# A graph network in four layers on one core: the third layer's convolution reads the adjacency as f32 strips for three query blocks at a time

## The chip, the core and the metric

The kernel runs on one NeuronCore of a Trainium2 chip. The engines are TensorE (PE, matmuls; PEld is its weight load), VectorE (DVE), ScalarE (ACT), GpSimd (POOL) and SyncE (SP); the last issues most of the transfers, and POOL issues those that change the type of the data. All transfers share the core's 16 DMA engines. The metric is the device time of one execution in microseconds (us); less is better. Three executions of the kernel before took 2046.96, 2052.23 and 2040.15 us.

## The reference

Four layers act on x (4096 nodes, 128 features) with one adjacency matrix adj (4096 x 4096, f32, symmetric, zeros and ones, ones on the diagonal). After each layer stands `x = layernorm(x + layer(x, adj))`.

Layer 0 is a hyperbolic layer with sigmoid attention, layer 1 a transformer convolution with four heads. The change is in layer 2, the third layer:

```python
def _L2_gnn_ref(x, adj, weight):
    n = adj.shape[0]
    adj_hat = adj + jnp.eye(n, dtype=adj.dtype)
    deg = jnp.sum(adj_hat, axis=1)
    d_inv_sqrt = (deg + 1e-08) ** (-0.5)
    support = d_inv_sqrt[:, None] * adj_hat * d_inv_sqrt[None, :]
    out = jnp.matmul(jnp.matmul(support, x), weight)
    return jax.nn.relu(out)
```

Layer 3 is a graph attention: `H = X @ W.T + b`, a score s_i + r_j for each edge, leaky_relu, softmax over the neighbours and `att @ H`. Layers 2 and 3 are in one function of the kernel, `layers23`.

## The kernel before

N is 4096, P is 128 (the partitions), S is 512 (a query block), NS = 8 blocks of nodes, NT = 32 tiles of 128 nodes, D = 128 features. X holds the features of all nodes in SBUF, node tiles on partitions. The order of a run is: layer 0 (0 to 700 us; in it `narrow`, L1917, writes a bf16 copy of adj, `adjb`, to DRAM by transfers of POOL that cast), completing the copy (to 790), layer 1 (to 1590), the convolution of layer 2 (to 1789), and layer 3, whose first block is `attend_first` (to 1829) and whose other seven are `attend_factored` (to the end).

`adjb` is stored in blocks of 512 x 512; `block(I, J)` is 128 partitions x 4 x 512 in bf16, 0.52 MB. The kernel takes fast paths that hold only if all entries of adj are zero or one. So it searches adj itself for other values: L1985 does this in layer 1 and `look` (L2336) in layer 2, each writing one column of marks per call (`mark`, up to MARKS columns). If a mark is set at the end, the whole net is run again by a general class; with these inputs it is not.

**The convolution.** Y holds the nodes scaled by deg^-1/2 in f32. `split` (L2353 on ACT, L2355 on DVE) takes it apart into three bf16 parts, each the rounded rest of the one before, for four tiles at a time. For a query block I and a block J of nodes, `convolve` (L2372) does 4 x 3 matmuls: node tile j of a part is the weights (128 x 128), the 512 columns of the adjacency block are the moving data, and everything is added up in one PSUM tile `pa` per query block. The order is I by I: 64 groups g = (I, J), each with one ring load from `adjb` on SP (`load`, L2322, ring of 8 blocks, seven ahead). The identity of `adj + I` is added by `diagonal` (L2346) to the block on the diagonal in the ring, or for the first block by identity matmuls (L2364).

The search is done beside it on f32 data of its own: `wide` (L2331) loads 1 MB halves of a strip of 128 rows of adj on SP into a pool `rot` of two buffers, and `look` is one instruction of 128 x 2048 on DVE, with every second group.

**The end of a query block** is `finish(I)`, a generator that is advanced one step a group beside the next query block: copy of the PSUM tile on ACT (L2401), the product with the weight on PE (pb, L2405), relu and scale on ACT (L2408), residual and layer norm on DVE (L2410 to L2419), transposes on PE (pt, L2425), and the scores of layer 3 (psr, L2443, `rho`, `col`, and the scaled features F, on PE, DVE and ACT). The sums over the own scores go over DVE (`urr`, L2432), in the last block over a matmul.

**The first attention block**, `attend_first`: for each of 32 node tiles one DVE instruction makes w from rho, col and the adjacency block (L2384), and an f32 matmul adds it to pa (L2387). It needs F and col of tile j, so the `finish` of block 7 must end before tiles 28 to 31; `close_first` gathers the sums and the marks. All this is inside `manual_schedule`, so each engine's order is the order of the program's text; SP and POOL take their issues in that order, and an issue that must wait for a buffer holds up those behind it on its queue.

The PSUM tiles are in pools `ps_b`, `ps_t`, `ps_s` and `ps_a` with two buffers each.

## Time and profile before

| | us |
|---|---|
| three executions, median | 2046.96 (2040.15 to 2052.23) |
| the profiled execution, its own time | 2050.21 |
| its span, first to last instruction | 2048.4 |
| layer 0, 0 to 700 | 700 |
| completing the bf16 copy, 700 to 790 | 90 |
| layer 1, 790 to 1590 | 800 |
| convolution of layer 2, 1590 to 1789 | 199, PE busy 187.2, DVE 147.9, DMA share 0.93 |
| first attention block, 1789 to 1829 | 40, PE busy 36.0, DVE 30.9, DMA share 0.36 |
| other seven blocks, 1829 to 2048 | 219, PE busy 207.5, DVE 185.5, DMA share 0.38 |

A line of the profile's groups reads: line of the kernel, engine, operation, what it writes and reads, shapes, count, then busy time in us and the mean ns of one, then the idle time of the engine ahead of them and what ended it. A line of a stretch reads: from and to, its length, busy time of PE, PEld, DVE, ACT and POOL with the number of instructions, the granted clock of TensorE as a share of full speed, the busy share of the 16 DMA engines, and the GB/s that they moved. The busy share of transfers can be over 1, since a packet's time counts while it waits. A line of the DMA issues gives the queue, how many, the size of one and the median time from issue to landing.

### The profile page before, as it was taken

To read this page: it belongs to the slowest core of one execution; us is meant where nothing else is said; L and a number is where in the kernel's file an instruction comes from. 1 tells how busy PE (TensorE), PEld (TensorE's weight loads), DVE (VectorE), ACT (ScalarE), POOL (GpSimd) and SP (SyncE) were. 2 spreads that over 40 slices of the span, in tenths; PEclk is the share of its full clock that TensorE was granted. 3 is DMA by queue.
4 is the path that set the end of the run, shared out by engine and by line. 5 is a ranking of instruction groups with operands and counts; after the bars stand their busy time and mean duration, and the time that the engine had idled before them with its cause. 6 is when DMAs were issued, how large, how long until landed. Compare 5 with 4: busy or idle time off the path is not lost.

```text
span 2048.4 us, 23818 instructions
## 1 busy us (share of the span) xinstructions
PE 1900.9 (93%) x8648; PEld 978.9 (48%) x8680; DVE 1736.6 (85%) x2685; ACT 1328.8 (65%) x1681; POOL 171.4 (8%) x269
## 2 busy tenths in 40 slices
PE   4789999999997788999999999999999799999997
PEld 4257766666666454333333333333333344444443
DVE  6579999998988946789999999999999777778986
ACT  5589999999997723777787777778787322210000
POOL 2211112111100221300000000000000000000000
PEclk8569999999999998999999999999999999999999
DMA  3488989899825977853535453545343799934441
GB/s 101 49 139 147 155 167 157 155 163 168 144 93 191 363 277 223 199 152 132 144 124 146 136 150 134 144 133 155 124 139 118 290 396 373 340 116 156 155 148 43
DMA packets 138064, 350.22 MB, mean 171 GB/s; under 512 B 13196, under 2 KB 56364, under 8 KB 125648
## 3 DMA queue, kind: packets, MB, share of 16 engines
q1 hardware_dynamic: 82944, 230.27, 32.3%
q0 software_dynamic: 45632, 50.69, 20.1%
q10 hardware_dynamic: 9360, 67.64, 9.9%
q8 instruction: 70, 1.15, 0.2%
q14 instruction: 58, 0.48, 0.1%
HBM read 371.54 MB, written 44.12 MB: 203 GB/s over the span
## 4 chain that ended last, share of the span: by engine, by line
PE 49%; DVE 24%; ACT 16%; DMA 6%; issue 4%; SPq 0%; POOL 0%; another core or an unknown queue 0%; ACTq 0%; DVEq 0%; POOLq 0%
PE pv L2020 11%; PE pa L1573 9%; DVE e L2003 9%; PE pa L2372 7%; PE ps L1994 6%; ACT e L2001 4%; PE pz L1775 3%; DMA up<-adjb 3%; DVE nat L1985 2%; ACT w L1792 2%; PE pi L1859 2%; PE pj L1874 2%; ACT s L1815 2%; ACT y L1811 2%; ACT y L1807 1%
## 5 line engine op out<-in xcount | busy, mean ns | idle before, releaser
L2003 DVE SCALAR_TENSOR_TENSOR e<-at,e 128x2048 f32<-128x2048 bf16 x256 | 582.6, 2286 | 77.3 <-ACT e L2001 76.7
L2001 ACT ACTIVATE e<-ps 128x1024 f32<-128x1024 f32 x512 | 492.9, 1024 | 150.6 <-PE ps L1994 121.6
L2020 PE MATMUL pv<-e,VA 128*64 128x512 f32 x2048 | 497.6, 607 | 6.7 <-DVE e L2003 5.7
L1994 PE MATMUL ps<-QS,KS 128*128 128x512 f32 x1024 | 314.8, 425 | 9.1 <-ACT e L2001 8.5
L1994 PEld LDWEIGHTS ps<-QS,KS 128*128 128x128 f32 x1024 | 170.9, 189 | 236.5 <-ACT e L2001 177.4
L2020 PEld LDWEIGHTS pv<-e,VA 128*64 128x64 f32 x2048 | 125.1, 136 | 250.2 <-issue 214.4
L1573 PE MATMUL pa<-w,Y 128*128 128x512 f32 x448 | 195.3, 594 | 0.0
L1775 PE MATMUL pz<-HT 128*128 128x512 f32 x288 | 171.8, 681 | 15.0 <-DVE w L1847 10.2
L1570 DVE SCALAR_TENSOR_TENSOR w<-rho,col,ring 128x512 f32<-128x512 f32 x224 | 162.7, 746 | 22.3 <-PE pa L1573 9.7
L2372 PE MATMUL pa<-ring,Y 128*128 128x512 bf16 x750 | 172.7, 384 | 8.7 <-ACT Y L2353 6.7
L1859 PE MATMUL pi<-HA,w 128*128 128x129 f32 x1152 | 156.6, 286 | 6.5 <-ACT s L1815 5.3
L1859 PEld LDWEIGHTS pi<-HA,w 128*128 128x128 f32 x1152 | 143.3, 199 | 18.2 <-issue 10.2
L1573 PEld LDWEIGHTS pa<-w,Y 128*128 128x128 f32 x448 | 83.8, 190 | 105.9 <-issue 80.3
L1976 ACT ACTIVATE nat<-nat 128x2048 f32<-128x2048 f32 x64 | 122.6, 1915 | 2.8 <-DMA nat<-in_adj_dram 2.8
L1874 PE MATMUL pj<-HA,w 128*128 128x129 f32 x896 | 120.7, 293 | 3.4 <-DVE X L1888 2.4
L2372 PEld LDWEIGHTS <-Y 128*128 128x128 bf16 x768 | 75.4, 99 | 100.9 <-ACT Y L2353 9.7
L1784 DVE TENSOR_SCALAR t<-pz 128x512 f32<-128x512 f32 x144 | 93.6, 682 | 30.2 <-PE pz L1778 30.2
L1874 PEld LDWEIGHTS pj<-HA,w 128*128 128x128 f32 x896 | 112.8, 205 | 11.2 <-issue 6.8
L1823 DVE SCALAR_TENSOR_TENSOR t<-t,s 128x2048 f32<-128x2048 f32 x36 | 82.3, 2286 | 13.4 <-ACT s L1815 13.4
L1792 ACT ACTIVATE w<-di,dr 128x512 f32<-128x512 f32 x144 | 90.6, 707 | 1.5 <-DMA di<-rows 1.5
L2336 DVE SCALAR_TENSOR_TENSOR nat<-nat 128x2048 f32<-128x2048 f32 x32 | 73.1, 2287 | 20.5 <-DMA nat<-in_adj_dram 20.5
L1847 DVE TENSOR_TENSOR w<-w,ptz 128x512 f32<-128x512 f32 x112 | 73.4, 681 | 18.7 <-PE ptz L1842 17.3
(410 smaller groups left out, 2343.1 us busy)
## 6 DMA issues: line engine op xcount, KB each, us to landing
nat<-in_adj_dram ACTq DMA_DIRECT2D x64, 1024.0 KB, 5.1
ring<-adjb SPq DMA_DIRECT2D x128, 512.0 KB, 4.7
ad<-in_adj_dram SPq DMA_DIRECT2D x36, 1024.0 KB, 9.4
adjb<-in_adj_dram POOLq DMA_DIRECT2D x64, 512.0 KB, 11.4
nat<-in_adj_dram SPq DMA_DIRECT2D x32, 1024.0 KB, 7.5
at<-adjb SPq DMA_DIRECT2D x63, 512.0 KB, 3.5
low<-adjb SPq DMA_DIRECT2D x36, 512.0 KB, 5.1
up<-adjb SPq DMA_DIRECT2D x28, 512.0 KB, 6.6
```

What stands on the lines that cost most here:

```text
L1570: nc.vector.scalar_tensor_tensor(w, rho[:, I * S : (I + 1) * S], col[:, 0, j : j + 1], at[:, jb, :], op0=ALU.max, op1=ALU.mult)
L1573: nc.tensor.matmul(pa, lhsT=F[:, j, :], rhs=w, start=False, stop=(j == NT - 1), skip_group_check=True)
L1775: nc.tensor.matmul(pz, lhsT=HT[:, j * P : (j + 1) * P], rhs=HT[:, I * S : (I + 1) * S], start=True, stop=False)
L1792: nc.scalar.activation(w[:, jb, :], st[p]["d"][k], AF.Sigmoid, bias=dr[:, 4 * J + jb : 4 * J + jb + 1])
L1859: nc.tensor.matmul(row[I, "po"][ib // 2][:, ib % 2, :], lhsT=st[p]["w0"][:, jb, ib * P : (ib + 1) * P], rhs=HA[:, 4 * J + jb, :], start=False,
L1874: nc.tensor.matmul(pj[:, a, :], lhsT=st[p]["w1"][:, ib, jb * P : (jb + 1) * P], rhs=HA[:, 4 * I + ib, :], start=(ib == 0), stop=(ib == 3),)
L1976: nc.scalar.activation(nat, nat, AF.Identity, accum_out=self.deg2[:, k, i : i + 1])
L1994: nc.tensor.matmul(p[:, h, :], lhsT=KS[:, h2 + h, jb * P : (jb + 1) * P], rhs=QS[I % 2][:, h2 + h, :], start=True, stop=True,)
L2001: nc.scalar.activation(e[:, h2 : h2 + 2, :], p, AF.Exp)
L2003: nc.vector.scalar_tensor_tensor(e, at[:, jb % 4, :].unsqueeze(1).to_broadcast([P, NH, S]), 0.0, e, op0=ALU.not_equal, op1=ALU.mult,)
L2020: nc.tensor.matmul(st["po"][h // 2][g : g + 64, :], lhsT=VA[:, o : o + 64], rhs=e[:, h, :], start=(jb == 0), stop=(jb == NT - 1), skip_gro ...
L2372: nc.tensor.matmul(st["pa"], lhsT=parts[k][:, j, :], rhs=at[:, jb, :], start=(I > 0 and j == k == 0), stop=(j == NT - 1 and k == 2), skip_ ...
```

## The change

The convolution no longer reads `adjb`. It reads adj itself, in strips: 128 rows of f32 and the columns of three query blocks (128 x 1536; in the last pass, with two query blocks, 128 x 1024), cast to F32R (a type in which TensorE takes f32 data with one matmul) by a transfer of POOL, `fetch`. There are three passes over the 32 row tiles, with query blocks 0 to 2, 3 to 5, and 6 and 7, 96 strips in all, in seven slots of which six are loaded ahead. A strip serves two parts of the nodes (F32R, `split` with two parts instead of three) and two or three query blocks, whose sums are in as many PSUM tiles (`ps_a` has four buffers now, `ps_b` and `ps_t` one).

The search uses the same strips: `look` runs two strips ahead of the matmuls on half of them (row tiles with j % 4 < 2, the same rows as before), and writes its unused result to a tile `junk` in bf16. The diagonal is added to the strip in the slot, 128 x 128. `wide`, `diagonal` and the identity matmuls are gone.

At the end of a pass the `finish` of two or three query blocks are opened together, and `proceed` advances one step a strip: the first alone, then the two at the head of the list by turns. After the last pass those of blocks 6 and 7 run beside `attend_first`, which goes tile by tile now; both of them take the sums by a matmul. The ring has six buffers, and its loads for the attention are issued in the last pass.

```diff
@@ -1643,7 +1643,7 @@
 
 class Fast(Net):
 
-    MARKS = 112
+    MARKS = 160
 
 
 
@@ -2250,7 +2250,9 @@
 
         nc, tc, N, NT, NS, D, X = self.nc, self.tc, self.N, self.NT, self.NS, self.D, self.X
         with ExitStack() as ctx:
-            RING = 8
+            RING, SLOTS = 6, 7
+            passes = [(0, 3), (3, 6), (6, 8)]
+            W = 3 * S
             ring = ctx.enter_context(tc.tile_pool(name="ring", bufs=1)).tile([P, RING, 4, S], BF16, tag="ring", name="ring")
             keep = ctx.enter_context(tc.tile_pool(name="keep3", bufs=1))
             pctx = ctx.enter_context(ExitStack())
@@ -2264,14 +2266,14 @@
             a0 = keep.tile([P, S], F32, tag="a0", name="a0")
             pre = pctx.enter_context(tc.tile_pool(name="pre3", bufs=1))
             rot = pctx.enter_context(tc.tile_pool(name="rot2", bufs=2))
+            slots = [pre.tile([P, W], F32R, tag=f"row{k}", name=f"row{k}") for k in range(SLOTS)]
+            junk = pre.tile([P, W], BF16, tag="junk", name="junk")
             wp = pctx.enter_context(tc.tile_pool(name="w2", bufs=4))
-            ps_b = pctx.enter_context(tc.tile_pool(name="ps_b", bufs=2, space=PSUM))
-            ps_t = pctx.enter_context(tc.tile_pool(name="ps_t", bufs=2, space=PSUM))
+            ps_b = pctx.enter_context(tc.tile_pool(name="ps_b", bufs=1, space=PSUM))
+            ps_t = pctx.enter_context(tc.tile_pool(name="ps_t", bufs=1, space=PSUM))
             ps_s = pctx.enter_context(tc.tile_pool(name="ps_s", bufs=2, space=PSUM))
-            ps_a = pctx.enter_context(tc.tile_pool(name="ps_a", bufs=2, space=PSUM))
-            parts = [pre.tile([P, NT, D], BF16, tag=f"Y{k}", name=f"Y{k}") for k in range(3)]
-            identb = pre.tile([P, P], BF16, tag="identb", name="identb")
-            nc.vector.tensor_copy(identb, self.ident)
+            ps_a = pctx.enter_context(tc.tile_pool(name="ps_a", bufs=4, space=PSUM))
+            parts = [pre.tile([P, NT, D], F32R, tag=f"Y{k}", name=f"Y{k}") for k in range(2)]
             w = self.load_mat(w2, "w2")
             br = self.load_row(bias, "br3", keep)
             wn = self.load_mat(weight, "wn3", pre)
@@ -2318,32 +2320,35 @@
                 nc.vector.memset(tot[:, D - 1 : D], float(N))
                 nc.vector.memset(eps, TINY)
 
-            def load(g):
-                nc.sync.dma_start(out=ring[:, g % RING, :, :], in_=self.block(g // NS % NS, g % NS))
+            def load(q):
+                nc.sync.dma_start(out=ring[:, q % RING, :, :], in_=self.block(q // NS, q % NS))
+
+            strips = [(lo, hi, j) for lo, hi in passes for j in range(NT)]
+
+            def fetch(n):
+
+                if n < len(strips):
+                    lo, hi, j = strips[n]
+                    nc.gpsimd.dma_start(
+                        out=slots[n % SLOTS][:, 0 : (hi - lo) * S], in_=self.adj[j * P : (j + 1) * P, lo * S : hi * S]
+                    )
 
             def open_sums():
                 return ps_a.tile([P, S], F32, tag="pa", name="pa")
 
-            def wide(n):
-
-                i, k = n // 4 * 4 + n // 2 % 2, n % 2
-                nat = st["nat", n] = rot.tile([P, N // 2], F32, tag="nat", name="nat")
-                nc.sync.dma_start(out=nat, in_=self.adj[i * P : (i + 1) * P, k * N // 2 : (k + 1) * N // 2])
-
             def look(n):
 
-                nat = st.pop(("nat", n))
-                nc.vector.scalar_tensor_tensor(
-                    nat, nat, 0.0, nat, op0=ALU.not_equal, op1=ALU.not_equal, accum_out=self.mark()
-                )
-
-            def diagonal(I):
-
-
-                at = ring[:, (NS * I + I) % RING, :, :]
-                for b in range(4):
-                    a = at[:, b, b * P : (b + 1) * P]
-                    nc.vector.tensor_tensor(a, a, identb, ALU.add)
+                lo, hi, j = strips[n]
+                a = slots[n % SLOTS]
+                if j % 4 < 2:
+                    w = (hi - lo) * S
+                    nat = a[:, 0:w].bitcast(F32)
+                    nc.vector.scalar_tensor_tensor(
+                        junk[:, 0:w], nat, 0.0, nat, op0=ALU.not_equal, op1=ALU.not_equal, accum_out=self.mark()
+                    )
+                if lo <= j // 4 < hi:
+                    o = j * P - lo * S
+                    nc.vector.tensor_tensor(a[:, o : o + P], a[:, o : o + P].bitcast(F32), self.ident, ALU.add)
 
             def split(J):
 
@@ -2351,54 +2356,45 @@
                 for k, part in enumerate(parts):
                     part = part[:, 4 * J : 4 * J + 4, :]
                     nc.scalar.copy(part, y)
-                    if k < 2:
-                        nc.vector.tensor_tensor(y, y, part, ALU.subtract)
-
-            def convolve(I, J):
-
-                if J == 0:
-                    st["pa"] = open_sums()
-                if I == J == 0:
-                    for b in range(4):
-                        for k in range(3):
-                            nc.tensor.matmul(
-                                st["pa"][:, b * P : (b + 1) * P], lhsT=parts[k][:, b, :], rhs=identb,
-                                start=(b == k == 0), stop=False, skip_group_check=True,
-                            )
-                at = ring[:, (NS * I + J) % RING, :, :]
-                for jb in range(4):
-                    j = 4 * J + jb
-                    for k in range(3):
+                    if k == 0:
+                        nc.vector.tensor_tensor(y, y, part.bitcast(F32), ALU.subtract)
+
+            def convolve(n):
+
+                lo, hi, j = strips[n]
+                for I in range(lo, hi):
+                    if j == 0:
+                        st["pa", I] = open_sums()
+                    for k in range(2):
                         nc.tensor.matmul(
-                            st["pa"], lhsT=parts[k][:, j, :], rhs=at[:, jb, :], start=(I > 0 and j == k == 0),
-                            stop=(j == NT - 1 and k == 2), skip_group_check=True,
+                            st["pa", I], lhsT=parts[k][:, j, :], rhs=slots[n % SLOTS][:, (I - lo) * S : (I - lo + 1) * S],
+                            start=(j == k == 0), stop=(j == NT - 1 and k == 1),
                         )
-            def attend_first(J):
-
-                if J == 0:
+
+            def attend_first(j):
+
+                if j == 0:
                     st["pa3"] = open_sums()
-                at = ring[:, (NS * NS + J) % RING, :, :]
-                for jb in range(4):
-                    j = 4 * J + jb
-                    t = wp.tile([P, S], F32, tag="w", name="w")
-                    nc.vector.scalar_tensor_tensor(
-                        t, rho[:, 0:S], col[:, 0, j : j + 1], at[:, jb, :], op0=ALU.max, op1=ALU.mult
-                    )
-                    nc.tensor.matmul(
-                        st["pa3"], lhsT=F[:, j, :], rhs=t, start=(j == 0), stop=False, skip_group_check=True
-                    )
+                at = ring[:, j // 4 % RING, :, :]
+                t = wp.tile([P, S], F32, tag="w", name="w")
+                nc.vector.scalar_tensor_tensor(
+                    t, rho[:, 0:S], col[:, 0, j : j + 1], at[:, j % 4, :], op0=ALU.max, op1=ALU.mult
+                )
+                nc.tensor.matmul(
+                    st["pa3"], lhsT=F[:, j, :], rhs=t, start=(j == 0), stop=False, skip_group_check=True
+                )
 
             def finish(I):
 
 
                 s, tl = slice(I * S, (I + 1) * S), slice(4 * I, 4 * I + 4)
                 x = X[:, tl, :]
-                a = rot.tile([P, S], F32, tag="a", name="a")
+                a = rot.tile([P, S], F32, tag="a", name="a", bufs=3)
                 o = rot.tile([P, 4, D], F32, tag="o", name="o")
                 rs = rot.tile([P, 4], F32, tag="rs", name="rs")
                 XT = rot.tile([P, S], F32, tag="XT", name="XT")
                 r = rot.tile([P, 4], F32, tag="r", name="r")
-                nc.scalar.copy(a, st["pa"])
+                nc.scalar.copy(a, st["pa", I])
                 yield
                 pb = ps_b.tile([P, 4, D], F32, tag="pb", name="pb")
                 for b in range(4):
@@ -2426,7 +2422,7 @@
                 nc.scalar.activation(XT, p.rearrange("p a b -> p (a b)"), AF.Identity, accum_out=part[:, I : I + 1])
                 nc.vector.tensor_tensor(XB[:, tl, :], x, br.unsqueeze(1).to_broadcast([P, 4, D]), ALU.add)
                 yield
-                if I < NS - 1:
+                if I < NS - 2:
                     ra = rot.tile([P, 4], F32, tag="ra", name="ra")
                     for b in range(4):
                         nc.vector.scalar_tensor_tensor(
@@ -2473,41 +2469,49 @@
                 nc.vector.tensor_scalar(self.good[:, 1:2], ma[0:1, :], LIMIT, None, op0=ALU.is_le)
                 nc.scalar.copy(tot[:, 0 : D - 1], p[0:1, 1, 0 : D - 1])
 
-            groups = NS * NS + NS
-            rest = iter(())
+            rest = []
+
+            def proceed():
+
+                while rest:
+                    r = rest.pop(0)
+                    if next(r, self) is not self:
+                        rest.insert(1 if len(rest) == 1 else 0, r)
+                        return
+
             with tc.manual_schedule():
-                for g in range(RING - 1):
-                    load(g)
+                for n in range(SLOTS - 1):
+                    fetch(n)
                 for J in range(2):
                     split(J)
-                    wide(J)
                 nc.scalar.preload_act_table_set("natural_log_exp_and_others")
-                for g in range(groups):
-                    I, J = g // NS, g % NS
-                    if g + 2 < NS:
-                        split(g + 2)
-                    if 0 < (g + 1) // NS == (g + 1) % NS < NS:
-                        diagonal((g + 1) // NS)
-                    if I < NS:
-                        convolve(I, J)
-                    else:
-                        attend_first(J)
-                    load(g + RING - 1)
-                    if g % 2 and g < NS * NS:
-                        look(g // 2)
-                        if g // 2 + 2 < NT:
-                            wide(g // 2 + 2)
-                    if g == 2:
+                for n in range(2):
+                    look(n)
+                for n, (lo, hi, j) in enumerate(strips):
+                    if lo == 0 and j % 4 == 0 and j // 4 + 2 < NS:
+                        split(j // 4 + 2)
+                    if n + 2 < len(strips):
+                        look(n + 2)
+                    convolve(n)
+                    fetch(n + SLOTS - 1)
+                    if n == 8:
                         weights()
-                    if g == 4:
+                    if n == 16:
                         weights_last()
-
-                    if J in (0, 1, 2, 3, 5, 6):
-                        next(rest, None)
-                    if J == NS - 1 and I < NS:
-                        rest = finish(I)
-                        next(rest)
-                    if g == groups - 2:
+                    if hi == NS and j % 5 == 0 and j // 5 < RING - 1:
+                        load(j // 5)
+                    if j:
+                        proceed()
+                    if j == NT - 1:
+                        rest = [finish(I) for I in range(lo, hi)]
+                        for r in rest:
+                            next(r)
+                for j in range(NT):
+                    attend_first(j)
+                    if j % 4 == 3:
+                        load(j // 4 + RING - 1)
+                    proceed()
+                    if j == NT - 5:
                         close_first()
                 nc.tensor.matmul(st["pa3"], lhsT=tot, rhs=eps, start=False, stop=True, skip_group_check=True)
                 nc.scalar.copy(a0, st["pa3"])
```

## The prediction

> **What bounds the kernel now.** The profiled execution took 2050.21 us by its own time, 1.8 above its span of 2048.4 and 3.3 above the median of the three runs (2046.96). I went first to the chain that ended last, where the line of the change, L2372, has 7%, then to the stretches around its stage. Columns: length, busy time of each engine, granted clock, DMA share, GB/s.
>
> ```profile
> PE 49%; DVE 24%; ACT 16%; DMA 6%; issue 4%; SPq 0%; POOL 0%; another core or an unknown queue 0%; ACTq 0%; DVEq 0%; POOLq 0%
> ```
> ```profile
> 1592.00:1600.00 8.00, 4.69 (x22) 2.22 (x24) 7.48 (x37) 5.10 (x8) 0.00 (x0) 0.79 0.93 323
> 1600.00:1630.00 30.00, 23.15 (x98) 9.97 (x99) 22.20 (x49) 11.21 (x22) 0.00 (x0) 0.89 0.78 289
> 1630.00:1660.00 30.00, 29.84 (x146) 14.95 (x148) 22.24 (x61) 6.47 (x22) 0.00 (x0) 1.00 1.01 414
> 1690.00:1720.00 30.00, 29.84 (x139) 14.41 (x141) 20.52 (x48) 7.01 (x23) 0.00 (x0) 1.00 0.96 372
> 1788.00:1830.00 42.00, 38.00 (x102) 16.56 (x100) 31.90 (x67) 6.04 (x19) 0.00 (x0) 0.96 0.38 125
> 1830.00:2048.00 218.00, 206.45 (x523) 92.83 (x521) 185.54 (x380) 6.75 (x16) 0.00 (x0) 0.98 0.38 126
> ```
>
> From 1630 to 1789 PE never rests, so PE sets the end of the convolution. But the DMA engines are full too, at 372 to 414 GB/s: a second bound lies directly under the first. That decides this case, because the change takes work from PE and no byte from the DMA. The groups in these stretches, and the issues with their landing times:
>
> ```profile
> L2372 PE MATMUL pa<-ring,Y 128*128 128x512 bf16 x750 | 172.7, 384 | 8.7 <-ACT Y L2353 6.7
> L1994 PE MATMUL ps<-QS,KS 128*128 128x512 f32 x1024 | 314.8, 425 | 9.1 <-ACT e L2001 8.5
> L2336 DVE SCALAR_TENSOR_TENSOR nat<-nat 128x2048 f32<-128x2048 f32 x32 | 73.1, 2287 | 20.5 <-DMA nat<-in_adj_dram 20.5
> ```
> ```profile
> ring<-adjb SPq DMA_DIRECT2D x128, 512.0 KB, 4.7
> ...
> adjb<-in_adj_dram POOLq DMA_DIRECT2D x64, 512.0 KB, 11.4
> nat<-in_adj_dram SPq DMA_DIRECT2D x32, 1024.0 KB, 7.5
> ```
>
> Then the order of time (start, length). A mean duration is not the rate of PE, as matmuls overlap: I use start to start. Fifteen bf16 matmuls fill 1659.75 to 1662.99, 0.216 each. Four F32R matmuls of the same 128x512 take 1.17 in all, the last of them 0.425: three steps of 0.25.
>
> ```profile
> 1659.75 3.40 PE L2372 MATMUL pa<-ring,Y 128*128 128x512 bf16 x15
> 1662.99 0.60 PE L2425 MATMUL pt<-ident,X 128*128 128x128 f32 x4
> ```
> ```profile
> 1007.14 1.17 PE L1994 MATMUL ps<-QS,KS 128*128 128x512 f32 x4
> ```
>
> **The change, part by part.**
>
> *PE.* Removed: 768 x 0.216 = 166 us. Added: 512 F32R matmuls x 0.25 = 128 (bounds 0.23 and 0.28: 118, 143). PE falls by 38, but a strip now needs 6 x 0.25 = 1.5 us (4 matmuls, 1.0, in the third pass) and its bytes need longer, as follows. PE is no longer the bound.
>
> *DMA.* Removed: 64 ring loads of 0.52 MB and 32 nat loads of 1.05 MB, 67.1 MB. Added: 64 strips of 0.79 MB and 32 of 0.52 MB, the same 67.1 MB. What moves is the path: from SP to POOL, because the transfer now casts f32 to F32R. No row shows such a transfer from 6 KB runs. The nearest:
>
> ```profile
> 766.00:776.00 10.00, 6.69 (x32) 5.91 (x32) 4.82 (x8) 2.61 (x4) 3.80 (x7) 0.67 1.15 382
> 892.00:898.00 6.00, 6.00 (x26) 2.32 (x24) 4.77 (x3) 4.59 (x6) 1.43 (x3) 1.00 1.32 216
> ```
>
> At 766 about half of the packets are F32R casts and half plain; at 892 nearly all are casts (KS and QS, 2 KB runs into 32 partitions). The packet records price it: an unhindered plain packet takes 84 ns for 2 KB, 159 for 4 KB, 309 for 8 KB, so 9 ns and 36.6 a KB; a cast one of 2 KB takes 98, 14 more. A 6 KB cast packet would take about 9 + 220 + 14 = 243 ns, which on 16 engines is 404 GB/s, a 4 KB one 379. I take 395 overall, between the 382 of the mixed stretch and the 414 of the plain one; ends for the range 216 and 414. At 395 the strips take 63.7 + 63.7 + 42.5 = 170 us, 1.99 a strip (1.33 in the third pass).
>
> The Trainium skill, "DMA: Bandwidth & Descriptors", sections Bandwidth and Rules for kernel authors, speaks against strips of this size: batch to 1 MiB or more, with 341 GB/s listed for a transfer of 1 MB from this queue and 425 for 16 MB. At 341 the 67.1 MB would take 197 us, 27 more than in my sum. The plain 0.5 MB ring loads of this trace ran at 414 with many in flight, so I do not take the figure of a lone transfer; no run here shows the cast queue with many.
>
> *Start.* In before the nat load waits for L2094, the last writer of layer 1, and starts at 1605.6; the first strip waits for the same. Two splits' subtractions (L2355, 0.69 each) and their waits stand ahead of L2094 in before and behind it now: I take 1601.9. Landings on this queue begin about 2 us after issue: the stream runs from 1603.9, where in before PE has convolved since 1596. The split's stalls of before (below, PE idle 4.4) go, and are worth nothing, as the strips are later than the split.
>
> ```profile
> 1605.63 0.81 SPq L2331 DMA_DIRECT2D nat<-in_adj_dram  x2
> ...
> 1610.94 2.29 DVE L2336 SCALAR_TENSOR_TENSOR nat<-nat 128x2048 f32<-128x2048 f32 x1 [4.07 <-DMA nat<-in_adj_dram]
> ...
> 1614.55 0.61 PE L2372 MATMUL pa<-ring,Y 128*128 128x512 bf16 x1 [4.42 <-ACT Y L2353]
> ```
>
> Six ring loads for the attention (3.1 MB) have no wait on SP and run before 1600, when the DMA has nothing else to do: nothing.
>
> *Slots.* A fetch waits on POOL for matmuls and search of the strip that had the slot; behind it stand only later fetches. POOL's 96 issues (0.75 each at L1917) are 72 us of 170: nothing. Six strips are ahead of PE, the search runs two ahead of it, so a DVE delay of four strips stops the stream.
>
> *DVE.* Search: 32 x 1.72 + 16 x 1.22 (L2336 by length) = 74.6 against 73.1. Diagonal: 32 x about 0.25. Split: 8 subtractions gone. A finish costs DVE 7.7 (its rows, 61.7 for eight). Pass 1 is free: 36 of 64 us. In pass 2 three finishes come in its first half: 16 x 0.95 + 24 = 39 us against 32 of transfer, 7 late, some absorbed by the lead: I take 4.5. In pass 3 it is 11 + 24 = 35 against 21: 14 late, the lead absorbs 5 and the second half 2: 6.5. Bounds 0 and 21 for both.
>
> *End of the convolution.* 1603.9 + 170 + 11 + about 1.8 for the last strip's landing and matmuls = 1786.7; before, 1789.4. So -2.7.
>
> *Attention of the first block.* Before 39.7 us (1789.4 to 1829.1), with one finish in it. Now two: the second adds 3.5 on PE (pb 1.05, pt 0.6, pr and psr 1.9) and 7.7 on DVE, whose 32 x 0.683 = 21.9 for w stand in the same queue; with them and single buffers for pb and pt I take +7 (bounds 3.5 and 11). The later stage is untouched; a ring of 6 leads by five blocks, 19 us of its 218, against a landing of 4.7: nothing.
>
> *Sum:* -2.7 + 7 = +4.3, 2054.5 for a profiled execution, some 2051 against the median; I say 2052.
>
> **The rivals.**
>
> 1. *Faster.* If the cast path keeps 414 and DVE keeps up, the stream ends at 1603.9 + 162 + 2 = 1768; with the attention's +7 that is -14, about 2033, and down to 2028 with +3.5. For it: DVE is busy 22 of 30 us in the windows above. Against: the finishes lie together. It needs the 11 us of stalls to be gone.
>
> 2. *Slower: the cast path is the bound.* At 355 the strips take 189 us, +19, less some 6 of DVE stalls that it hides: 2065. At 330: 203 us, 2077. The 892 stretch's 216 would make it 311 us, about 2180; against this end: those transfers fill 32 partitions with 2 KB runs. From about 375 GB/s down the kernel is slower by more than 0.5% (10 us, about what a measurement can tell from no change).
>
> 3. *Slower: DVE and the finish chain are the bound.* If the three finishes hold the search as one block, the 21 us of lateness go into the path whole and the attention takes +11: 2066. For it: a finish hands over between PE, ACT and DVE six times. Against: its steps are spread one a strip.
>
> 4. *Slower clock.* The granted clock was 0.89 where PE was busy 77% (1600 to 1630), and PE will now be at 70%. A strip's 1.5 would be 1.7, still under 1.99; it counts only in the attention and after stalls: +3, inside my range.
>
> **How the numbers follow.** Forecast with 382 to 414 GB/s and stalls of 5 to 15: 0.45 (2043 to 2060: 0.36 within 0.5%, 0.07 slower, 0.02 faster). Rival 1: 0.15, of it 0.13 faster, 0.02 within. Rival 2: 0.22 between 330 and 360, slower; 0.05 near 216, slower. Rival 3: 0.13, of it 0.11 slower, 0.02 within. Faster 0.15, same 0.40, slower 0.45. The range leaves out the 216 case and the ends of rivals 1 and 2: 2031 to 2080; the forecast's own is 2043 to 2060.
>
> **What would show it.** Right: L2369's matmuls start near 1608 and end near 1787, DMA share near 1 at about 395 GB/s from 1605 on, PE busy about 75% and waiting for the row DMA in pass 1 and for the diagonal or the DMA in passes 2 and 3; POOL waiting for the look in the first halves of these; the attention about 47 us. Wrong: a DMA share near 1 at 355 or less (rival 2), DVE busy over 95% from 1670 (rival 3), or PE busy at 100% with the stage over before 1775 (rival 1).

## The result

The changed kernel took 2064.28 us (median of eight executions, 2058.56 to 2073.24) against 2048.24 (eight, 2040.15 to 2052.23): a ratio of 1.0087, with a 95% interval of 1.0065 to 1.0110. That is slower by about 18 us, more than the 0.5% that a measurement can tell from no change. The forecast, 2052, was 12 us too low; its range held the time and its own narrower one (2043 to 2060) did not. The profiled execution took 2062.37 us, 1.8 above its span of 2060.6.

The chain, the same groups and the issues in the profile after, each with its own view:

```profile
PE 40%; DVE 27%; ACT 17%; DMA 11%; issue 6%; POOL 0%; SPq 0%; ACTq 0%; DVEq 0%; POOLq 0%
```
```profile
L2369 PE MATMUL pa<-row,Y 128*128 128x512 f32 x512 | 141.4, 426 | 35.0 <-DVE row L2351 30.1
...
L2346 DVE SCALAR_TENSOR_TENSOR junk<-row 128x1536 bf16<-128x1536 f32 (+1 forms) x48 | 75.7, 1578 | 45.0 <-DMA row<-in_adj_dram 44.4
```
```profile
row<-in_adj_dram POOLq DMA_DIRECT2D x64, 768.0 KB, 9.3
```

The convolution's matmuls now idle 35.0 us ahead of them (8.7 before), 21.7 of it the late start, and the DMA has 11% of the chain (6% before). The stretches are the three passes, the first attention block and the rest:

```profile
1603.00:1671.00 68.00, 53.85 (x204) 39.54 (x205) 37.70 (x62) 10.41 (x17) 20.74 (x39) 0.88 1.07 397
1671.00:1738.70 67.70, 55.88 (x234) 41.10 (x233) 50.70 (x132) 13.83 (x47) 16.70 (x33) 0.97 1.03 369
1738.70:1791.60 52.90, 43.02 (x171) 31.58 (x170) 43.04 (x130) 13.94 (x48) 13.80 (x26) 0.90 0.87 289
1791.60:1842.00 50.40, 41.55 (x116) 18.07 (x114) 36.73 (x84) 9.61 (x33) 0.00 (x0) 0.90 0.24 84
1842.00:2060.60 218.60, 207.41 (x525) 93.16 (x524) 185.57 (x380) 7.61 (x17) 0.00 (x0) 0.98 0.39 130
```

No engine is full in any pass, the DMA runs at its pace only in the first, and the last stage is as before (219.3). In the packet records of pass 1 most strips of 0.79 MB land 1.88 us after the one before, which is 418 GB/s.

The end of layer 1 falls between 1582 and 1597 us in the profiles of this study, though its code is the same, so stages are counted from the end of its last ev copy (L2033; 1590.4 before, 1588.3 after). "Start" is the time from there to the first matmul of the convolution that reads the adjacency (the identity matmuls of the kernel before, from 0.6 on, are left out); a pass ends where the last copy of its sums begins. All in us from one profiled execution each; the ratio is that of the timed runs to the kernel before.

| kernel | start | pass 1 | pass 2 | pass 3 | first block | ev copy to end | ratio (95%) |
|---|---|---|---|---|---|---|---|
| before | 5.7 | 193.2, no passes | | | 39.8 | 458.0 | 1 |
| changed | 22.3 | 59.7 | 68.4 | 52.9 | 50.4 | 472.3 | 1.0087 (1.0065 to 1.0110) |
| look_late | 22.3 | 58.8 | 67.6 | 51.1 | 54.1 | 472.5 | 1.0065 (1.0034 to 1.0096) |
| no_look | 20.7 | 60.7 | 60.5 | 48.5 | 54.6 | 463.8 | 1.0025 (1.0004 to 1.0046) |
| reorder | 22.6 | 60.8 | 67.6 | 52.1 | 53.3 | 474.9 | 1.0112 (1.0082 to 1.0143) |
| one_part | 22.3 | 59.2 | 67.0 | 51.4 | 56.3 | 474.8 | 1.0079 (1.0048 to 1.0109) |
| turns | 22.3 | 61.4 | 67.8 | 49.8 | 53.9 | 474.0 | 1.0069 (1.0038 to 1.0099) |
| turns_reorder | 22.6 | 59.7 | 65.9 | 51.5 | 53.2 | 471.4 | 1.0076 (1.0054 to 1.0098) |
| attend_slow | 22.7 | 59.2 | 68.4 | 53.1 | 49.9 | 471.9 | 1.0091 (1.0055 to 1.0126) |
| warm | 22.6 | 60.5 | 68.6 | 53.9 | 57.7 | 481.9 | 1.0106 (1.0070 to 1.0142) |
| early | 12.1 | 63.7 | 69.7 | 52.5 | 53.8 | 469.9 | 1.0043 (1.0013 to 1.0073) |
| late_rho | 22.5 | 61.2 | 65.9 | 52.2 | 46.5 | 466.9 | 1.0054 (1.0036 to 1.0073) |
| early_late | 12.0 | 63.2 | 66.6 | 51.0 | 46.9 | 457.8 | 1.0001 (0.9980 to 1.0023) |
| all_three | 12.4 | 64.3 | 64.6 | 48.0 | 47.4 | 454.9 | 0.9999 (0.9982 to 1.0015) |

Two spreads are needed to read it. Passes 2 and 3 together took 121.3 to 122.5 us in the four profiles that have the same code there (changed, attend_slow, warm, early). The first block took 50.4 to 56.3 in the eight that have the same code there (changed to turns_reorder, and early). The layers before are not in these numbers, but they are in the timed runs: in reorder the profiled execution was the fastest of five (2059.47 against a median of 2073.06), though its stages are no shorter.

The +14.3 of the two profiles is +4.5 up to the end of the convolution, +10.6 in the first block and -0.7 after it. The bytes alone need 60.2 + 60.2 + 40.1 = 160.5 us at 418 GB/s; passes 2 and 3 take 21.0 more than that.

### The profile page after: what moved, and what is told of

It is laid out like the page before. It is cut to its first block, busy times and chain, and to the rows that moved or that the text cites. A ratio compares the mean times of both kernels' runs of the same rounds, so it can differ in the third digit from the quotient of the medians.

```text
span 2060.6 us, 23409 instructions
## 1 busy us (share of the span) xinstructions
PE 1862.3 (90%) x8420; PEld 994.1 (48%) x8420; DVE 1738.7 (84%) x2704; ACT 1323.2 (64%) x1673; POOL 222.8 (11%) x365
## 3 DMA queue, kind: packets, MB, share of 16 engines
q8 instruction: 68, 1.11, 0.2%
## 4 chain that ended last, share of the span: by engine, by line
PE 40%; DVE 27%; ACT 17%; DMA 11%; issue 6%; POOL 0%; SPq 0%; ACTq 0%; DVEq 0%; POOLq 0%
PE pv L2020 10%; PE pa L1573 9%; DVE e L2003 9%; PE ps L1994 6%; ACT e L2001 4%; DMA row<-in_adj_dram 3%; DMA up<-adjb 3%; ACT w L1792 3%; PE pz L1775 2%; DVE nat L1985 2%; ACT s L1815 2%; PE pj L1874 2%; ACT y L1811 2%; DVE t L1823 2%; PE pi L1859 2%
## 5 line engine op out<-in xcount | busy, mean ns | idle before, releaser
L2001 ACT ACTIVATE e<-ps 128x1024 f32<-128x1024 f32 x512 | 493.1, 1024 | 150.5 <-PE ps L1994 123.4
L1994 PE MATMUL ps<-QS,KS 128*128 128x512 f32 x1024 | 315.1, 426 | 10.9 <-ACT e L2001 10.2
L2369 PE MATMUL pa<-row,Y 128*128 128x512 f32 x512 | 141.4, 426 | 35.0 <-DVE row L2351 30.1
L2369 PEld LDWEIGHTS pa<-row,Y 128*128 128x128 f32 x512 | 99.6, 202 | 70.3 <-issue 28.0
L1874 PEld LDWEIGHTS pj<-HA,w 128*128 128x128 f32 x896 | 109.5, 200 | 12.1 <-issue 6.8
L2346 DVE SCALAR_TENSOR_TENSOR junk<-row 128x1536 bf16<-128x1536 f32 (+1 forms) x48 | 75.7, 1578 | 45.0 <-DMA row<-in_adj_dram 44.4
L2332 POOL DMA_DIRECT2D row<-in_adj_dram x96 | 51.2, 536 | 350.1 <-DMA ac<-in_L_gnn_a_r_dram 220.6
```

The lines of the kernel that those rows point to most:

```text
L1874: nc.tensor.matmul(pj[:, a, :], lhsT=st[p]["w1"][:, ib, jb * P : (jb + 1) * P], rhs=HA[:, 4 * I + ib, :], start=(ib == 0), stop=(ib == 3),)
L1994: nc.tensor.matmul(p[:, h, :], lhsT=KS[:, h2 + h, jb * P : (jb + 1) * P], rhs=QS[I % 2][:, h2 + h, :], start=True, stop=True,)
L2001: nc.scalar.activation(e[:, h2 : h2 + 2, :], p, AF.Exp)
L2369: nc.tensor.matmul(st["pa", I], lhsT=parts[k][:, j, :], rhs=slots[n % SLOTS][:, (I - lo) * S : (I - lo + 1) * S], start=(j == k == 0), sto ...
```

## The experiments

Three accounts of the 21 us stood against each other: DVE has too much work where the finishes come (theory 1), its work or the finish's steps stand in the wrong order or too close (theories 2 and 4), or the cast path and POOL set the pace (called rival 3 in the expectations below; it is rival 2 of the prediction). For the first block it was the spacing (5a), the amount (5b), the pause at psr (5c) or the clock (6), and for the late start the memory that the slots lie on (7).

### Is it DVE's search? no_look, look_late, reorder

The search left out (the diagonal stays):

```diff
-                if j % 4 < 2:
+                if False:
```

> The changed kernel without the search of the third layer (48 instructions of 128x1536 and 128x1024 on DVE); it leaves out the search of those strips for values other than zero and one. Theory 1 and theory 2: DVE has only three finishes of 8 us in passes 2 and 3, the stalls of 21 us go, passes 2 and 3 take 60 and 40 us: 17 to 22 us less, 2042 to 2047. Rival 3 (cast path or POOL): passes stay at 67 and 55 us, no change.

2053.38 us, 13 us less by the ratios; pass 2 fell to 60.5, the time of its bytes. Pass 3 fell from 52.9 only to 48.5. The three passes without the search:

```profile
1608.00:1668.70 60.70, 53.19 (x201) 37.91 (x201) 8.64 (x27) 7.25 (x13) 16.39 (x31) 0.94 1.11 418
1668.70:1729.20 60.50, 55.54 (x235) 40.18 (x236) 24.03 (x99) 14.45 (x49) 17.13 (x33) 1.00 1.11 416
1729.20:1777.70 48.50, 42.87 (x171) 28.38 (x169) 23.93 (x97) 13.92 (x48) 13.54 (x26) 0.96 0.93 316
```

416 GB/s through all of pass 2 excludes the cast path and POOL's issues as the cause of the 68.4 us. So the stall of pass 2 needs the search, and two thirds of that of pass 3 (8.4 of 12.8) do not. The total gain was below what either theory said, because pass 3 kept 8.4 and the first block, whose code is the same, took 54.6 (below).

Next, only the place of the search in DVE's queue:

```diff
-                    if n + 2 < len(strips):
-                        look(n + 2)
                     convolve(n)
...
                     if j:
                         proceed()
+                    if n + 2 < len(strips):
+                        look(n + 2)
```

> The changed kernel with one move: the search of strip n+2 is put behind the matmuls of strip n and the finish step instead of ahead of them, so on DVE a finish step that is ready no longer stands behind a search that waits for its strip. The changed kernel took 1.0087 of the kernel before (about 2064 us); its passes 2 and 3 are some 21 us longer than their transfers at 418 GB/s. Theory 1 (the amount of DVE work: search and three finishes together exceed the transfer time of half a pass): within 4 us of the changed kernel, 2060 to 2066. Theory 2 (the order: a waiting search holds up a finish, whose transposes hold up PE's queue, as in the 4.70 us wait for DVE X at 1684): 8 to 12 us less, 2052 to 2056. Rival 3 (the cast path or POOL's issues set passes 2 and 3): no change.

Passes 2 and 3 lost 2.6 us together. Theory 2, that the order alone is the cause, falls; it has at most a small part. Then the order of the strips, in passes 2 and 3 the 16 without a search first:

```diff
-            strips = [(lo, hi, j) for lo, hi in passes for j in range(NT)]
+            late = [j for j in range(NT) if j % 4 > 1] + [j for j in range(NT) if j % 4 < 2]
+            strips = [(lo, hi, j) for lo, hi in passes for j in (late if lo else range(NT))]
```

> The changed kernel with the strips of passes 2 and 3 in another order: the 16 that are not searched first, beside the finishes, then the 16 that are searched. No work is added or taken away. Theory 1: DVE has 24 us in the first half and 27 (20 in pass 3) in the second, against 30 (20 in pass 3) of transfer: of the 21 us of stalls 12 to 17 go, 2047 to 2052, about the kernel before. Theory 2: the same 12 to 17, since no search stands ahead of a finish. Rival 3: no change, 2064.

Nothing was gained: 67.6 and 52.1. That is rival 3's number, but no_look had excluded its cause. It is not the number of theory 1 or 2, which both said that 12 to 17 us would go. The trace of this order suggests why (second half of pass 2):

```profile
1700.00:1716.00 16.00, 9.56 (x41) 7.23 (x39) 15.62 (x39) 4.20 (x14) 3.70 (x7) 0.88 1.07 388
1716.00:1733.00 17.00, 16.26 (x60) 13.07 (x61) 16.34 (x25) 0.55 (x2) 4.38 (x9) 0.82 0.94 319
```

DVE is busy 31.96 of 33 us. Sixteen searches at 1.8 in a row, the diagonals and the tail of the finishes are more than the 30 us of 16 strips' transfer. The expectation had put 27 there and forgotten the tail. PE is busy as well, 16.26 of the last 17 us at a clock of 0.82, but it had waited 7.2 us for one diagonal within these 33. So theory 1 can stand, by a reckoning made after the run: the collision is moved by this order, not dissolved. What is shown by a run is that 12.3 of the 21 us go with the search.

### Is PE still a bound? one_part

```diff
-                    for k in range(2):
+                    for k in range(1):
```

> The changed kernel with only the first part of the nodes in the convolution: 256 matmuls instead of 512, which leaves out the second part of the sum. PE falls by 60 to 70 us. If PE is no longer the bound, as predicted, 0 to 6 us less than the changed kernel (quicker after a stall): 2058 to 2064. If PE (matmuls with a weight load each, at a clock of 0.84 to 0.92 after idle time) still sets the passes, 15 us less or more: under 2049.

Half of the matmuls gone, and the ratio is 1.0079 (1.0048 to 1.0109): no measurable difference, as predicted. Passes 2 and 3 lost 2.9 us together, and the first block took 56.3. PE's busy time in the three passes fell only from 152 to 120 us, at a clock of 0.65 to 0.86; even so PE was idle for 58 us of the 178, and nothing was gained.

### Is it the latency of the finish? turns, turns_reorder

In the changed kernel a finish takes one step a strip. When DVE is late, PE stands at the transposes of that step, and the convolution behind it; the slots are not given back. Pass 2 of the changed kernel (start, length, engine, what; idle before and releaser):

```profile
1677.96 1.64 PE L2369 MATMUL pa<-row,Y 128*128 128x512 f32 x6 [0.23 <-DMA row<-in_adj_dram]
1678.01 1.76 DVE L2346 SCALAR_TENSOR_TENSOR junk<-row 128x1536 bf16<-128x1536 f32 x1 [3.90 <-DMA row<-in_adj_dram]
...
1682.22 1.75 DVE L2346 SCALAR_TENSOR_TENSOR junk<-row 128x1536 bf16<-128x1536 f32 x1
...
1683.89 1.12 DVE L2415 TENSOR_SCALAR X<-X,mv,rs 128x128 f32<-128x128 f32 x4
1684.29 1.25 PE L2421 MATMUL pt<-ident,X 128*128 128x128 f32 x4 [4.70 <-DVE X L2415]
...
1688.41 0.53 POOL L2332 DMA_DIRECT2D row<-in_adj_dram  x1 [7.57 <-PE pa L2369]
```

DVE waits 3.90 for a strip, then has two searches and a layer norm to do; PE waits 4.70 for that, and POOL 7.57 for PE's slots. Here the transfer is at its pace up to the moment when the finish comes, and the finish stops it. The test gives each finish a step in every third strip:

```diff
                     r = rest.pop(0)
                     if next(r, self) is not self:
-                        rest.insert(1 if len(rest) == 1 else 0, r)
+                        rest.append(r)
                         return
```

(o, rs, r and ra get three buffers, and XT takes the place of a, which is free by then.)

> The changed kernel with the three finishes of a pass advanced in turns, so that two steps of one finish are three strips apart instead of one (the tiles that three open finishes need have three buffers). Same work on every engine. Theory 4 (latency: a finish step that comes one strip after the last one makes PE's queue wait for DVE or ACT, the pt for DVE X and the pb for ACT o, and the convolution stands behind it): the PE waits of 12.8 us on finish steps in passes 2 and 3 mostly go, pass 2 falls from 68.5 to 61 to 64, pass 3 from 53 to 43 to 48; 9 to 15 us less than the changed kernel, 2050 to 2055. Theory 1 (amount of DVE work in the first half of a pass): passes 67 and 52, 0 to 3 us less.

Pass 2 67.8, pass 3 49.8: 3.7 less together, not the 9 or more that theory 4 needs. PE's waits for X fell from 10.0 to 5.5 us, but those for the diagonal (L2351, in the same DVE queue) rose from 7.5 to 9.5. With the strips reordered as well:

> Both edits, the finishes in turns and the unsearched strips first in passes 2 and 3. Alone the second gave nothing (pass 2 67.6, pass 3 52.5 us). Theory 4: with no search between them the steps are never late: pass 2 60 to 62, pass 3 41 to 45; 13 to 18 us less than the changed kernel, 2046 to 2051. Theory 1: the DVE amount was settled by the reorder, which gained nothing, so nothing here either: 2060 to 2068.

65.9 and 51.5. PE waited 7.42 us at one place, again for a diagonal behind searches in a row. Theory 4 is a part of it, some 4 us (5.0 in the last kernel below); both tests fell short of what it foresaw. The 8.4 us of pass 3 that remain without search lie where the finishes run: in the packet records of no_look the strips of this pass land 1.28 us apart, but seven in its first half come 1.7 to 2.9 apart, together 7 us late. How they split between the steps of the finish stays open; no run isolates them.

### The first attention block: attend_slow, warm, late_rho

Two finishes lie in it instead of one. First their steps were spread, 14 over 24 tiles instead of 14:

```diff
-                    proceed()
+                    if (j + 1) * 14 // 24 > j * 14 // 24:
+                        proceed()
```

> The changed kernel with the 14 finish steps inside the first attention block spread over 24 tiles instead of 14. Same work. The block takes 50.4 us (39.7 before). Theory 5a (steps too close together: DVE does both finishes first while PE waits 1.3 to 2.2 us per tile): 43 to 47 us. Theory 5b (the amount: one finish more costs 7.7 us of DVE wherever it lies): 48 to 51. In total 4 to 7 us less, or 0 to 2.

49.9 us, and the same time in all, not the 43 to 47 that 5a needs. PE stood idle for 8.1 us of the block, against 8.9 in the changed kernel and up to 9.4 in the others with its code, so the spacing is worth about 1 us at most: 5a falls as the main cause. The clock was the second suspect; in the changed kernel it reads, in two stretches of the block:

```profile
1799.60:1803.60 4.00, 2.48 (x3) 1.02 (x4) 3.90 (x14) 0.41 (x2) 0.00 (x0) 0.66 0.20 79
1815.60:1819.60 4.00, 1.78 (x3) 0.84 (x3) 3.79 (x8) 2.32 (x8) 0.00 (x0) 0.50 0.00 0
```

The test added work to PE, two matmuls behind each of the first 14 tiles:

```diff
                     attend_first(j)
+                    for _ in range(2 if j < 14 else 0):
+                        nc.tensor.matmul(st["warm"], lhsT=parts[0][:, j, :], rhs=slots[0][:, 0:S], start=True, stop=True)
```

> The changed kernel with 28 matmuls more in the first attention block, two after each of its first 14 tiles, whose results nobody reads: 28 x 0.23 = 6.4 us more of PE, placed where PE waits for DVE. Theory 6 (the granted clock falls to 0.5 after such waits, 0.66 and 0.50 in two stretches of 4 us, and that lengthens the PE-bound work that follows): the clock stays at 1, the block becomes 2 to 6 us shorter, 45 to 48. Rival (the clock has no part in it): 1 to 6 us longer, 51 to 56.

57.7 us. In this form theory 6 failed: the matmuls lie beside the tiles, but the pauses come after psr, and there the clock fell to 0.50 all the same. (In the first half, where the added matmuls shortened the pauses to 0.85 and 1.61 us, it stayed at 1.00 and did not fall to 0.66.) The trace of no_look, whose block has the code of the changed kernel, shows the pause twice (second occurrence):

```profile
1802.79 2.05 PE L2439 MATMUL psr<-XT,us 128*128 128x512 f32 x2
1807.06 18.55 PE L2383 MATMUL pa<-w,Y 128*128 128x512 f32 x36 [2.22 <-DVE w L2380]
```

The two matmuls of psr took 2.05 us here, at a clock of 0.50, and 1.10 at the first occurrence (1796.02), at 1.00. In the step of psr DVE waits for PE, and then the next w stands behind rho on DVE while PE waits for w. The kernel before shows this pause once in its block:

```profile
1817.01 5.40 PE L2387 MATMUL pa<-w,Y 128*128 128x512 f32 x8 [2.22 <-DVE w L2384]
```

The remedy lets one tile pass between the two:

```diff
                 nc.tensor.matmul(ps, lhsT=us, rhs=XT, start=True, stop=True)
-
+                yield "again"
                 nc.vector.tensor_scalar(r, ra[:, 0:4], cb[:, 1:2], 2.0 * LIMIT, op0=ALU.add, op1=ALU.min)
...
-                    if next(r, self) is not self:
-                        rest.insert(1 if len(rest) == 1 else 0, r)
+                    v = next(r, self)
+                    if v is not self:
+                        rest.insert(0 if v == "again" else 1 if len(rest) == 1 else 0, r)
```

> The changed kernel with one more step in each finish: what DVE and ACT do with the scores (from r, L2441, on) comes one strip or tile after the matmul psr instead of in the same step. Same work. Theory 5c (the bubble: in the step of psr DVE waits for PE about 2 us and then PE waits 2.2 us for the w tile that stands behind rho on DVE; the kernel before has one such bubble in the first attention block, the changed kernel two, and the clock is 0.5 after the second): the block falls from 50.4 to 42 to 46, passes 2 and 3 together by 2 to 4 us; 6 to 12 us less in all, 2052 to 2058. Theory 5b (the amount of DVE work): block 49 to 52, 0 to 3 us less.

46.5 us, a little above the 42 to 46 expected, and 46.9 and 47.4 in the two kernels below that have it too; the nine profiles with the old step, warm left out, lie between 49.9 and 56.3. The block in the kernel before and here, and what is left of the two pauses here:

```profile
1789.30:1829.10 39.80, 35.80 (x94) 15.64 (x93) 30.60 (x64) 5.18 (x17) 0.00 (x0) 0.96 0.35 120
```
```profile
1795.90:1842.40 46.50, 39.38 (x115) 17.29 (x113) 36.13 (x84) 9.53 (x33) 0.00 (x0) 0.96 0.27 91
```
```profile
1816.65 1.13 PE L2383 MATMUL pa<-w,Y 128*128 128x512 f32 x2 [1.37 <-DVE w L2380]
...
1821.75 14.00 PE L2383 MATMUL pa<-w,Y 128*128 128x512 f32 x32 [1.36 <-DVE w L2380]
```

The pauses are shorter, 1.4 us instead of 2.2, and the clock is 1.00 from 1809 to the end of the block. Against the changed kernel PE's idle time in the block fell by 1.7 us (8.85 to 7.12) and its busy time, for the same matmuls, by 2.2 (41.55 to 39.38). So theory 5c holds for the block, and more of the gain comes over the clock than from the pauses themselves. In all it is 1.0054 against 1.0087, 7 us, though these two intervals overlap; the median of 2060.55 is above the 2052 to 2058 expected. Passes 2 and 3 lost 3.2.

### The late start: early

In the changed kernel the first fetch and the first matmul are these:

```profile
1603.37 3.77 POOL L2332 DMA_DIRECT2D row<-in_adj_dram  x7 [220.59 <-DMA ac<-in_L_gnn_a_r_dram]
...
1610.63 1.62 PE L2369 MATMUL pa<-row,Y 128*128 128x512 f32 x3 [21.66 <-DVE row L2351]
```

In the experiment the slots and the parts are allocated ahead of the other tiles:

```diff
+            first = ctx.enter_context(tc.tile_pool(name="first", bufs=1))
+            slots = [first.tile([P, W], F32R, tag=f"row{k}", name=f"row{k}") for k in range(SLOTS)]
+            parts = [first.tile([P, NT, D], F32R, tag=f"Y{k}", name=f"Y{k}") for k in range(2)]
             ring = ctx.enter_context(tc.tile_pool(name="ring", bufs=1)).tile([P, RING, 4, S], BF16, tag="ring", name="ring")
...
-            slots = [pre.tile([P, W], F32R, tag=f"row{k}", name=f"row{k}") for k in range(SLOTS)]
...
-            parts = [pre.tile([P, NT, D], F32R, tag=f"Y{k}", name=f"Y{k}") for k in range(2)]
```

> The changed kernel with the seven slots and the two parts allocated ahead of all other tiles of layers 2 and 3, so that they lie on memory that layer 1 gives back before its last normalisation: the first fetch then waits for the last PV matmul of layer 1 (L2020) instead of L2094, the split for no work of layer 1's end. Same work. In the changed kernel the convolution starts 22.4 us after the last ev copy of layer 1, in the kernel before 5.6. Theory 7 (the late start is lost as a whole, since the stream is the bound in pass 1): start at 7 to 11, 11 to 15 us less than the changed kernel, 2049 to 2053. Rival (the stalls of pass 2 and 3 swallow it, or the layer-1 end is slowed by the stream): 0 to 5 us less.

The first fetch went out at 1591.12 instead of 1603.37, the convolution started at 12.1 instead of 22.3, and 5.3 us of the 10.2 were left at its end; the ratio is 1.0043 (1.0013 to 1.0073), 9 us less with overlapping intervals. Both ends of the expectation were partly right. In this kernel DVE stands at the first search, ahead of layer 1's normalisation:

```profile
1591.12 3.77 POOL L2333 DMA_DIRECT2D row<-in_adj_dram  x7 [207.28 <-DVE Y L2361]
...
1598.87 1.76 DVE L2347 SCALAR_TENSOR_TENSOR junk<-row 128x1536 bf16<-128x1536 f32 x1 [5.71 <-DMA row<-in_adj_dram]
```

Layer 1's last L2094 started at 1618.7, 29.5 after the ev copy (about 12 in the changed kernel), and pass 1 took 63.7.

### Together: early_late, all_three

> Both edits, the early slots and the later use of the scores. They act in different places, so theories 7 and 5c together give 17 to 27 us less than the changed kernel, 2037 to 2047, which would be under the kernel before; if one of them fails 2049 to 2058; if both, 2060 to 2066.

2051.91 us, 1.0001: the loss is gone, the kernel is where the kernel before is, but not under it, and the 2037 to 2047 expected of both edits were not reached. The two profiles differ by 14.5 us from the ev copy to the end, close to the 17 to 18 of the ratios. With the finishes in turns added:

> The changed kernel with the early slots, the later use of the scores, and the finishes in turns. The first two together gave 1.0001 of the kernel before (12.1 us to the start, attention 47.0); the third shortened pass 3 from 53 to 49.8 us by itself. If it does so beside them: 3 to 5 us under the kernel before, 0.997 to 0.999. If the stalls only move (DVE's work in the first half of a pass is the same), 0.999 to 1.002.

From the ev copy to the end it took 454.9 us in its profile, 3.1 less than the kernel before, and passes 2 and 3 lost another 5.0, but the timed runs gave 0.9999 (0.9982 to 1.0015). No version here is measurably faster than the kernel before.

## Why the prediction was right and wrong

**What bounds the stage: right for pass 1.** PE's relief brought nothing (one_part), and the bytes set the pace of pass 1. In passes 2 and 3 they did not; the stalls below came on top.

**Rate of the cast path: too low.** 395 was taken, 418 measured. A 6 KB packet took 248 ns in the packet records against the 243 that were worked out; the three plain packets of the prediction (84, 159 and 309 ns) give 37.5 ns a KB and not 36.6, and with that it comes to 248. One such packet at a time on each of 16 engines would be 396 GB/s; that 418 were moved, at a DMA share of 1.07 to 1.11, says that the packets of an engine overlap. The low rate gave the sum 170 us for 160.5, 9.5 too much. Rival 2 fell with it. The Trainium skill's "DMA: Bandwidth & Descriptors" (section Bandwidth) lists 341 GB/s for a transfer of 1 MB from this queue; strips of 0.79 MB with six in flight went at 418 here, near the 425 that it lists for 16 MB.

**Start: too early.** From the ev copy, the first fetch was put at 11.5 and came at 15.1. L2094's end was about as late as assumed (1600.4, 12.1 after the ev copy); POOL's last wait for layer 1 ended at 1600.61 and its first issue began at 1603.37. The profile puts this gap down to a load on SP, on which the fetch has no wait; what fills it is open. Another 1.6 us is the search of the first strip, which stands ahead of its diagonal on DVE: without the search the start is 20.7. I had not questioned the size of the whole term: 16.6 us later than before, beside the stalls the largest cost of the change. Another place for the tiles brought the start 10.2 earlier (early), and 5.3 of that were left at the end of the convolution.

**Stalls of DVE in passes 2 and 3: the step that failed.** 4.5 + 6.5 = 11 were taken, of 0 to 21; 21.0 came. The reckoning credited a lead of four strips. It does not protect, because the same late DVE step stops PE in its own queue (4.70 above), and PE's matmuls free the slots. So rival 3, where "the 21 us of lateness go into the path whole", is what happened, at 0.13. That its 2066 is so close to the 2064 measured is in part luck: it holds the same 9.5 us too much for the bytes and the same start that is too early. In passes 2 and 3 alone the higher rate hid 5.9 of the 10 us that the stalls were too small by. I had argued against rival 3 that the steps are spread one a strip; three strips apart (turns) took back only some 4 of the 21.

**First attention block: too small.** +7 was taken, +10.6 came in the profile, near the bound of 11, and up to +16 in other profiles with the same code. The 3.5 of PE fits: late_rho, at the clock of before, has PE busy for 39.38 us against 35.80. The 7.7 of DVE was somewhat high as an amount (busy 36.7 against 30.6); missing was the pause behind psr, which the trace of before showed once (PE 2.22 idle at 1817.01) and which comes once for each finish. Of the +10.6, PE's idle time is 4.9 (4.0 to 8.9) and its busy time 5.8.

**Clock: rival 4 was counted as +3.** In the block it is 0.79 to 0.90 in the profiles with the old step and 0.93 to 0.96 in the three with the later use of the scores. The longer blocks have the lower clock: PE's idle time in the nine profiles with the old step is 8.1 to 9.4 us, while its busy time for the same matmuls goes from 41.6 to 47.5. Of the +10.6 the clock is about 2.2 (41.55 busy against the 39.38 of late_rho). No run changes the clock alone; warm, which was to do so, did not.

In sum, from the ev copy and against the prediction (pass 2 63.7 + 4.5, pass 3 42.5 + 6.5, and so pass 1 to 79.1): start and pass 1 +2.9, pass 2 +0.2, pass 3 +3.9, first block +3.7, the rest -0.7, together 10.0 more than the forecast +4.3. In the start and pass 1 the higher rate made up for a part of the later fetch.

## What to carry to other kernels

When work is taken from the engine that is full and a second resource lies just under it, reckon the gain from the second one's time, and then look for what stops that stream: here steps of an in-order queue that wait for a busy engine. Buffers that are loaded ahead are no cover if the engine that frees them waits in the same chain. Two things were worth the loss here and cost no work: a step between a matmul and its reader on an engine that also feeds PE, and tiles that are needed first on memory that comes free first.

## What the runs showed that I had not expected

- F32R casts in transfers of POOL with 6 KB runs moved 418 GB/s, as much as plain transfers did in the kernel before (414); the 216 GB/s stretch of layer 1 said nothing about them.
- In the first attention block the clock fell to one half with pauses of PE of 2.07 to 2.23 us, or within 3 us of them (changed, no_look, late_rho, kernel before) and not with those of 0.85 to 1.61 (warm, late_rho). The matmuls that followed took longer: psr 2.05 us instead of 1.10. Blocks with the same code took 50.4 to 56.3 us, at a mean clock of 0.90 and 0.79.
- POOL's first issue came 2.76 us after its last wait for layer 1 had ended.
